# Two alternating parts at the join of layers 1 and 2, and layer 3's norms by a power on GpSimd

## The chip, the cores and the metric

The kernel runs on one core of a Trainium2 chip. The core has TensorE (PE, with its weight loads PEld), VectorE (DVE), ScalarE (ACT) and GpSimd (POOL); SyncE (SP) issues the DMAs. Each engine has its own queue of instructions and takes them in order; semaphores make one wait for another. SBUF holds the tiles, PSUM (eight banks) what PE writes, HBM the rest. The metric is the device time of one launch in microseconds (us), the median of the runs.

## What is computed

Four images of 128 channels and 64 x 64 pixels go through four layers. The parts that the change touches, cut from the reference:

```python
x = x + L0(_gn(x))                 # sorted patches, a scan over 4096 tokens, put back in place
x = x + L1_conv(_gn(x))            # 3x3 convolution of the group norm
t = tokens(x)                      # (B, 4096, 128)
t = t + L2_attn(_ln_t(t))          # 16 heads of 8
t = t + L2_ffn(_ln_t(t))
t = t + L3_attn(_ln_t(t))          # linear attention
t = t + L3_ffn(_ln_t(t))

def L2_attn(x):                    # x is already a layer norm
    q = _qz_ring(heads(x) + rx_theta)
    ctx = softmax(q q^T / sqrt(8)) q
    x1 = _ln(x + ctx @ w_comb.T + b_comb, g1, beta1)
    h = relu((cos(x1[..., :8]) * cos(ry_theta)) @ w1.T + b1)
    return _ln(x1 + h @ w2.T + b2, g2, beta2)

def _ln_t(v, eps=1e-5):
    m, s = mean(v, -1), var(v, -1)
    return (v - m) / sqrt(s + eps)
```

L2_attn's first part, up to `ctx`, is "attention" below; what comes after it, from the division by the softmax's sums to the last norm, is the "feed-forward".

## The kernel before

A batch is held as 128 channels by 4096 tokens and worked through in 8 chunks of 512. Matmuls in float32 go through PE in two passes, so that one line of code can show as two instructions in the trace. Nearly all matmuls have the line of the helper `mm`, L92, and many deferred steps that of `later`, L137; tiles' names tell them apart.

**Order.** Outside two blocks whose order is written out by hand (the scan of layer 0, and the attention of layer 2 for PE, DVE and POOL), a scheduler orders each engine's instructions when the kernel is built: among those that its model holds ready, the one that stands first in the program. A tile waits for its buffer, and a pool opened where another was waits for the tiles that it covers.

**Layers 0 and 1** (`layers01`, from L277). The scan over all batches runs to about 2637 us. Beside it, other batches are prepared or ended. `end` (L1024) is the end of one batch: load the image `xb` in four DMAs, put the scan's output back in place (`put_back`, L962: transposes `perm_t`, matmuls `perm_p` with a permutation, adds into `xb`), then `convolve` (L1001: group norm, 16 pieces of 18 matmuls `conv`, an add each, four stores to `xd`). It is a generator of about 53 turns; `K.flush()` after each turn issues the steps that it deferred, and `K.banks` says how many PSUM banks it may use. The last batch's end runs alone, after the scan, in a pool of eight banks (L1075 to L1081).

**Layer 2** (`layer2_attention`, L1112). First constants: 18 small DMAs on SP and some work on DVE (L1124 to L1183). For each batch then: `prepare` (L1228), in 8 chunks of six stages, `fetch` (load `x_in` from `xd`), `centred` and `norm` (the two halves of a layer norm), `products`, `running` (cosines and their products), `store` (values into `qt` and `value_d`, heads into `head_d`); then `load_steps` reads the first head's keys and queries back in 32 DMAs and POOL rounds them (L1218, L1226). `attention` (L1328) needs all eight PSUM banks and runs its heads one after the other; in each it loads the next head's keys and queries. A part of each head's sums goes to `around_d` by one DMA (L1444). `feed_forward` (L1566) works off the batch before in nine stages a chunk; `fetch` loads `den`, `num` and `nrm_in`, `divisors` (L1609) turns the softmax's sums by matmuls with `pick`, `first_centred` (L1629) adds the residual by a matmul with `center`. The two chunks that need `around_d` come last, and `gathered` (L1584) reads it for each in 16 DMAs of 8 rows. `in_turn` sets the stages of the chunks against each other, and `in_turns` takes one step of each part in each round. For batch b, the feed-forward of b - 1, its `gathered` part, and `prepare(b)` with its loads run together, in this order within a round.

**Layer norm** (`layernorm_steps`, L100). PE centres a chunk; ACT squares it and keeps a copy; PE takes the mean of the squares; DVE transposes (L116); ACT takes the square root (L118); DVE the reciprocal (L119); PE spreads it by transposes (L122); DVE multiplies (L124). ACT holds one table of functions; an `ACT_TABLE_LOAD` comes before a function of another table. `layernorm` (L94) runs all of it in one go and is used by layer 3's attention alone (`norm`, L1999); its chunks go through `norm`, `keys`, `add`, and beside them those of the batch before through `queries`, `weighed`, `give`. The experts' part has another form already: `weigh` adds epsilon on DVE and takes the power -0.5 on POOL (L1796, L1800).

Of the kernel before, what the change touches and what calls it, by code (L numbers as in the profile page):

```python
# [17 lines left out]
P = 128  # L18
# [12 lines left out]
class Common:  # L31
# [62 lines left out]
    def layernorm(self, out, src, work, psum):  # L94


        for _ in self.layernorm_steps(out, [(self.center, src)], work, psum):
            pass

    def layernorm_steps(self, out, terms, work, psum, affine=None, bufs=2):  # L100
# [7 lines left out]
        nc.scalar.activation(sq, xc, AF.Square, bias=shift)  # L108
        kept = work.tile([P, CH], F32, name="ln_kept", bufs=bufs)
        nc.scalar.activation(kept, xc, AF.Identity, bias=shift)  # L110
# [6 lines left out]
        sd = work.tile([P, 4, 1], F32, name="ln_sd")  # L117
        nc.scalar.activation(sd, vt[:, :, 0:1], AF.Sqrt, bias=self.eps5)  # L118
        nc.vector.reciprocal(sd, sd)  # L119
        by_block = vp.rearrange("p (g b i) -> p b g i", b=4, i=32)  # L120
        for k in range(4):
            nc.tensor.transpose(by_block[:, k], sd[:, k].to_broadcast([P, P]), self.ident)  # L122
# [154 lines left out]
def layers01(K, xd, dpool, w, w1):  # L277
# [9 lines left out]
    with ExitStack() as ctx:  # L287
        pool = lambda name, bufs, **kw: ctx.enter_context(tc.tile_pool(reuse_waits="tile", name=name, bufs=bufs, **kw))
        cst = pool("l0_const", 1)
        big = pool("l0_big", 1)  # L290
        small = pool("l0_small", 1)

        norm_g = column(nc, cst, w["norm_g"], "norm_g")
        norm_b = column(nc, cst, w["norm_b"], "norm_b")
        conv1_b = column(nc, cst, w["conv1_b"], "conv1_b")
        conv2_b = column(nc, cst, w["conv2_b"], "conv2_b")
        ca1_wT = matrix(nc, cst, w["ca1_wT"], "ca1_wT")
        ca2_wT = matrix(nc, cst, w["ca2_wT"], "ca2_wT")
        head_w = column(nc, cst, w["head_w"], "head_w")
        head_b = rows(nc, cst, w["head_b"], "head_b")  # L300
        nc.vector.tensor_scalar(head_b, head_b, 0.5, None, ALU.mult)
        z_projT = matrix(nc, cst, w["in_proj_wT"][:, 256:512], "z_projT")
        conv1d_b = column(nc, cst, w["conv1d_b"], "conv1d_b", 2)
        dt_projT = matrix(nc, cst, w["dt_proj_wT"], "dt_projT")
        dt_b = column(nc, cst, w["dt_proj_b"], "dt_b", 2)

        a_neg = cst.tile([P, NQ, NG], F32, name="a_neg")
        for z in range(2):
            for q in range(NQ):
                nc.sync.dma_start(  # L310
                    out=a_neg[64 * z : 64 * z + 64, q, :].unsqueeze(2),
                    in_=w["A_log"][64 * q : 64 * q + 64, :].rearrange("d (g z) -> d g z", z=2)[:, :, z : z + 1],
                )
        d_skip = column(nc, cst, w["D"], "d_skip", 2)
        out_projT = matrix(nc, cst, w["out_proj_wT"], "out_projT", 2)
        taps = cst.tile([P, 9, P], F32, name="taps")
        nc.sync.dma_start(out=taps, in_=w1["weightT"])
        bias = column(nc, cst, w1["bias"], "bias")

        x_projT = cst.tile([P, 2, 80], F32, name="x_projT")  # L320
        nc.vector.memset(x_projT, 0.0)
        for at, rows_ in ((0, slice(0, 24)), (64, slice(24, 40))):
            nc.sync.dma_start(
                out=x_projT[:, :, at : at + rows_.stop - rows_.start],
                in_=w["x_proj_wT"].rearrange("(k p) f -> p k f", k=2)[:, :, rows_],
            )

        row32 = K.shifted("row32_0", K.row_i, 1, (31, None, ALU.bitwise_and))
        state = cst.tile([32, DS], F32, name="state")
        nc.vector.tensor_scalar(state, K.col[0:32, 8 : 8 + DS], row32[0:32], None, ALU.is_equal)  # L330
        c_d = dpool.tile([2, DS, CH], F32, name="c_d")
        image_d = [dpool.tile([P, (HW + 2) * (HW + 2)], F32, name=f"image_d{i}") for i in range(2)]
        y_d = [dpool.tile([P, L], F32, name=f"y_d{b}") for b in range(NB - 2)]

        pair = cst.tile([P, 64], F32, name="pair")
        nc.vector.tensor_tensor(pair, K.ident[:, 0:64], K.ident[:, 64:128], ALU.add)

        in_projT = small.tile([P, 256], F32, name="in_projT", tag="rank_eq")
        nc.sync.dma_start(out=in_projT, in_=w["in_proj_wT"][:, 0:256])
        taps1d = cst.tile([P, 4, 256], F32, name="taps1d")  # L340
        nc.sync.dma_start(out=taps1d, in_=w["conv1d_wT"].partition_broadcast(P))
        nc.vector.tensor_tensor(
            taps1d, taps1d, in_projT.unsqueeze(1).to_broadcast([P, 4, 256]), ALU.mult
        )
        nc.scalar.activation(a_neg, a_neg, AF.Exp)
        nc.vector.tensor_scalar(a_neg, a_neg, -1.0, None, ALU.mult)
        head_bc = cst.tile([P, 64], F32, name="head_bc")
        nc.vector.tensor_scalar(head_bc, K.ones[:, 0:64], head_w, None, ALU.mult)

# [65 lines left out]
        def together(*parts):  # L415

            parts = list(parts)
            while parts:
# [3 lines left out]
                if parts:  # L422
                    yield
# [1738 lines left out]
```

## Time and profile before

| what | us |
|---|---|
| median of the runs (9740.41 to 9745.49) | 9741.62 |
| the profiled execution, its own time | 9744.07 |
| its span, first to last instruction | 9742.2 |
| layers 0 and 1, to the scan's end | 2637 |
| last batch's end, then constants and preparation of batch 0, to the first key load | 2637 to 2847.7 |
| first key load to the first exponential of attention | 2847.7 to 2886.65 |
| attention of batch 0 | 2886.65 to 4168.4 |
| feed-forward of a batch with the next one's preparation, three times | 207, 203, 203 |
| last feed-forward alone | 8627 to 8772 |
| layer 3's attention | 9068 to 9457 |
| granted TensorE clock over the span | 0.927 of full |

A row of the timeline has the start, the length, the engine, the line of code, the instruction, the tile written and the tiles read, the count, and in brackets how long the engine had been idle and what released it. SPq is SP's queue of DMA issues: its lengths are the time to issue, not to land. A row of a line's answer has the count and the shortest, median and longest duration in ns, then the first and last start. Matmuls' ends are modelled.

### The profile page before, as it was taken

Reading aid. Unit: us, or ns where it says so; the run is one execution under the profiler, and the core shown is the slowest. Engines: PE = TensorE matmul, PEld = TensorE weight load, DVE = VectorE, ACT = ScalarE, POOL = GpSimd, SP = SyncE. Lnnn points to the kernel's source line nnn. Section 1 sums busy time; section 2 is a strip of 40 time slices with the busy share of each in tenths; the row PEclk is TensorE's granted clock in tenths of the full one; section 3 lists DMA queues with packets and bytes.
Section 4 is the critical chain, followed back from the end, with each engine's and each line's share of the span. In section 5 each row is a group of like instructions: output and inputs, shape, how many; then the busy total and the mean of one; then the engine's idle time right before and its main releaser. Section 6 shows DMA issues by size and latency. Waiting matters only on the chain.

```text
span 9742.2 us, 188843 instructions
## 1 busy us (share of the span) xinstructions
PE 8688.3 (89%) x74586; PEld 3347.3 (34%) x74586; DVE 7104.0 (73%) x7782; ACT 7404.1 (76%) x10635; POOL 4901.3 (50%) x3255
## 2 busy tenths in 40 slices
PE   5887878889859999979999979999979999987777
PEld 2222222234433333333333333333333333333443
DVE  1889897987738888858888857888867888853454
ACT  3776767654439999969999969999979999972442
POOL 1677676765525555545555545555545555542001
PEclk8887888889879999989999989999989999998898
DMA  4524435222232222142212232222233222224105
GB/s 117 124 72 113 102 80 130 61 66 82 73 73 38 40 39 40 31 109 41 39 40 40 38 96 51 40 39 40 39 91 57 39 40 40 40 57 134 44 10 165
DMA packets 575734, 635.37 MB, mean 65 GB/s; under 512 B 113080, under 2 KB 369152, under 8 KB 573824
## 3 DMA queue, kind: packets, MB, share of 16 engines
q1 hardware_dynamic: 574848, 623.30, 27.4%
q8 instruction: 588, 9.63, 0.4%
q14 instruction: 298, 2.44, 0.1%
HBM read 446.84 MB, written 109.07 MB: 57 GB/s over the span
## 4 chain that ended last, share of the span: by engine, by line
PE 68%; DVE 10%; POOL 7%; ACT 5%; DMA 5%; issue 4%; SPq 1%; DVEq 0%; POOLq 0%; ACTq 0%
PE ctx_ps L92 27%; PE acc_ps L92 14%; PE score L92 11%; DVE hs L919 4%; PE conv L92 4%; POOL hs L923 3%; DVE hs L908 2%; PE y_ps L92 2%; PE ln_xc L92 1%; PE xc_ps L92 1%; PE b_ps L92 1%; DMA w<-in_L_ffn_weight 1%; PE kv L92 1%; ACT decay L915 1%; ACT L915 1%
## 5 line engine op out<-in xcount | busy, mean ns | idle before, releaser
L1542 ACT ACTIVATE ex<-score 128x1024 f32<-128x1024 f32 x5120 | 4925.1, 1036 | 224.6 <-PE score L92 133.2
L92 PE MATMUL ctx_ps<-ex,qt 128*32 128x512 f32 x20480 | 2733.7, 606 | 19.9 <-DVE ctx L1476 19.9
L1491 POOL TENSOR_TENSOR folded<-ex 128x1024 f32<-128x1024 f32 x512 | 1224.0, 2391 | 2100.7 <-ACT ex L1542 1836.1
L1548 DVE STREAM_TRANSPOSE turned<-ex 128x1024 f32<-128x1024 f32 x1536 | 1885.2, 1227 | 335.1 <-ACT ex L1542 334.7
L1524 DVE STREAM_TRANSPOSE turned<-ex 128x1024 f32<-128x1024 f32 x1532 | 1841.8, 1202 | 0.0
L92 PE MATMUL acc_ps<-turned,turned_v 128*32 128x256 f32 x24576 | 1769.5, 379 | 3.1 <-POOL qt L1236 2.3
L919 DVE TENSOR_TENSOR_SCAN hs<-decay,carry,hs 128x512 f32<-128x512 f32 x1024 | 1245.4, 1265 | 196.5 <-ACT decay L915 183.5
L92 PE MATMUL score<-queries,keys 32*128 32x512 f32 x10240 | 1335.4, 497 | 50.0 <-POOL queries L1226 45.3
L92 PEld LDWEIGHTS acc_ps<-turned,turned_v 128*32 128x32 f32 x24576 | 800.9, 110 | 1476.5 <-issue 1324.1
L923 POOL TENSOR_TENSOR hs<-hs,c_sb 128x1024 f32<-128x1024 f32 x512 | 1207.2, 2358 | 70.9 <-DMA c_sb<-c_d 28.6
L915 ACT ACTIVATE decay<-dt,a_neg 128x512 f32<-128x512 f32 x1024 | 693.0, 689 | 656.7 <-DVE hs L919 644.1
L92 PEld LDWEIGHTS score<-queries,keys 32*128 32x128 f32 x10240 | 512.6, 182 | 1145.2 <-ACT ex L1542 780.8
L1354 POOL TENSOR_TENSOR turned_v<-v,quarter 128x1024 f32<-128x1024 f32 x256 | 612.8, 2394 | 264.5 <-PE acc_ps L92 227.1
L92 PE MATMUL y_ps<-hs,pair 128*64 128x512 f32 x2048 | 655.7, 768 | 32.1 <-POOL hs L923 32.1
L1492 POOL TENSOR_TENSOR quarters<-folded 128x512 f32<-128x512 f32 x512 | 658.0, 1285 | 40.2
L92 PEld LDWEIGHTS ctx_ps<-ex,qt 128*32 128x32 f32 x20480 | 406.3, 108 | 654.7 <-issue 598.7
L908 DVE TENSOR_TENSOR hs<-dtx,b_ps 128x2048 f32<-128x2048 f32 x256 | 579.7, 2264 | 54.2 <-PE b_ps L92 30.2
L92 PE MATMUL b_ps<-dbc,state 32*64 32x512 f32 x1024 | 341.2, 748 | 235.0 <-DVE hs L908 234.9
L922 POOL COPY carry<-hs 128x2 f32<-128x2 f32 x512 | 97.9, 191 | 684.0 <-DVE hs L919 665.5
L1542 ACT ACTIVATION_READ_ACCUMULATOR ex<-score 128x1 f32 x2048 | 436.2, 213 | 0.0
L1476 DVE COPY ctx<-ctx_ps 128x512 f32<-128x512 f32 x256 | 176.8, 691 | 329.4 <-PE ctx_ps L92 327.1
L1533 DVE TENSOR_REDUCE dacc<-quarters 128x2 f32<-128x512 f32 x508 | 326.8, 643 | 0.0
(375 smaller groups left out, 8943.8 us busy)
## 6 DMA issues: line engine op xcount, KB each, us to landing
c_sb<-c_d SPq DMA_DIRECT2D x512, 128.0 KB
queries<-head_d SPq DMA_DIRECT2D x1024, 64.0 KB
keys<-head_d SPq DMA_DIRECT2D x1024, 64.0 KB
under<-image_d SPq DMA_DIRECT2D x192, 264.0 KB
dt<-dt SPq DMA_DIRECT2D x128, 256.0 KB
dtx<-dtx SPq DMA_DIRECT2D x128, 256.0 KB
v<-value_d SPq DMA_DIRECT2D x1024, 32.0 KB
w<-in_L_ffn_weight SPq DMA_DIRECT2D x32, 1024.0 KB
```

What stands on the lines that cost most here:

```text
L92: self.nc.tensor.matmul(out, lhsT, rhs, start=start, stop=stop)
L908: nc.vector.tensor_tensor(hs, dtx2, bb.unsqueeze(1).to_broadcast([P, NQ, CH]), ALU.mult)
L915: nc.scalar.activation(ex, dt2[:, q, :], AF.Exp, scale=a_neg[:, q, g : g + 1])
L919: nc.vector.tensor_tensor_scan(hs[:, q, :], decays[q - 2 * i], hs[:, q, :], carry[:, g, q : q + 1], ALU.mult, ALU.add)
L923: nc.gpsimd.tensor_tensor(hs[:, two, :], hs[:, two, :], cs.unsqueeze(1).to_broadcast([P, 2, CH]), ALU.mult)
L1354: nc.gpsimd.tensor_tensor(t, v.unsqueeze(2).to_broadcast([P, 4 * BT, 4, HD]), quarter.unsqueeze(1).to_broadcast([P, 4 * BT, 4, HD]), ALU.mult,
L1491: nc.gpsimd.tensor_tensor(hs, exs[:, :, 0], exs[:, :, 1], ALU.add)
L1492: nc.gpsimd.tensor_tensor(qs, hs[:, :, 0 : CH // 2], hs[:, :, CH // 2 :], ALU.add)
L1524: nc.vector.transpose(*upright)
L1533: nc.vector.tensor_reduce(at, qs, AX.X, ALU.add)
L1542: nc.scalar.activation(ex, sps[p], AF.Exp, scale=scale, accum_out=sums[:, t : t + 1] if summed else None)
L1548: nc.vector.transpose(*upright)
```

## The change

It has five parts. (1) The last batch's end is returned as a generator `last()` and runs alternately with the preparation of batch 0, a turn of the one and a step of the other; each has four PSUM banks, and layer 2's constants and large tiles are taken from the other side of SBUF. The constants now stand before the last batch's end in the program. Loads of the first head come after both. (2) `layernorm` takes the root by `inverse_root`: an add of epsilon on DVE and a power on POOL. (3) The feed-forward adds the residual on DVE (`more`) instead of PE, turns the sums by transposes and a reduction, and its parts come after `prepare` and its loads in a round. (4) `gathered` begins 12 rounds later and reads `around_d` in two DMAs of 120 and 8 rows. (5) For this, the first 15 heads of a batch store to `around_d` in 16 DMAs of 8 rows each.

The diff is large because a `with` block was dissolved and its lines moved to the left; without that:

```diff
-        for _ in self.layernorm_steps(out, [(self.center, src)], work, psum):
+        for _ in self.layernorm_steps(out, [(self.center, src)], work, psum, power=True):
...
-        nc.scalar.activation(sq, xc, AF.Square, bias=shift)
         kept = work.tile([P, CH], F32, name="ln_kept", bufs=bufs)
-        nc.scalar.activation(kept, xc, AF.Identity, bias=shift)
+        if more is not None:
+            nc.vector.scalar_tensor_tensor(kept, xc, shift, more, ALU.add, ALU.add)
+            nc.scalar.activation(sq, kept, AF.Square)
+        else:
+            nc.scalar.activation(sq, xc, AF.Square, bias=shift)
+            nc.scalar.activation(kept, xc, AF.Identity, bias=shift)
...
-        nc.scalar.activation(sd, vt[:, :, 0:1], AF.Sqrt, bias=self.eps5)
-        nc.vector.reciprocal(sd, sd)
+        if power:
+            self.inverse_root(sd, vt[:, :, 0])()
+        else:
+            nc.scalar.activation(sd.unsqueeze(2), vt[:, :, 0:1], AF.Sqrt, bias=self.eps5)
+            nc.vector.reciprocal(sd, sd)
...
-            K.banks = 8
-        with (
-            tc.tile_pool(reuse_waits="tile", name="l0_last", bufs=2) as work,
-            tc.tile_pool(reuse_waits="tile", name="l0_ps", bufs=8, space=PSUM) as psum,
-        ):
+    work = pool("l0_last", 2)
+    psum = pool("l0_ps", 4, space=PSUM)
+    K.banks = 4
-            for _ in end(NB - 1, seqs[NB - 1], work, psum):
-                K.flush()
-            K.flush()
-            K.flush()
+    def last():
+        for _ in end(NB - 1, seqs[NB - 1], work, psum):
+            K.flush()
+            yield
+        K.flush()
+        K.flush()
+    return last(), ctx
...
+def one_by_one(*parts):
+    for part in parts:
+        yield from part
...
-        cst = pool("l2_const", 1)
-        keep = pool("l2_keep", 2)
+        cst = pool("l2_const", 1, side="right")
+        keep = pool("l2_keep", 2, side="right")
...
-                    nc.sync.dma_start(out=around_d[h], in_=accs[h][:, 0].rearrange("p t r -> p (t r)"))
+                    sums = accs[h][:, 0].rearrange("p t r -> p (t r)")
+                    if h + 1 < NH:
+                        for k in range(16):
+                            r = slice(HD * k, HD * k + HD)
+                            nc.sync.dma_start(out=around_d[k, HD * h : HD * h + HD], in_=sums[r])
+                    else:
+                        nc.sync.dma_start(out=around_last_d, in_=sums)
...
-                for h in range(NH):
-                    nc.sync.dma_start(
-                        out=part[HD * h : HD * h + HD],
-                        in_=around_d[h, :, c * P : (c + 1) * P].rearrange("(n d) f -> d n f", d=HD),
-                    )
-                    if h % 4 == 3:
-                        yield
-                yield
+                cols = slice(c * P, (c + 1) * P)
+                r = HD * (NH - 1)
+                nc.sync.dma_start(out=part[0:r], in_=around_d[:, 0:r, cols].rearrange("n q f -> q n f"))
+                nc.sync.dma_start(out=part[r:], in_=around_last_d[:, cols].rearrange("(n d) f -> d n f", d=HD))
+                yield from [None] * 4
...
             def firsts():
+                yield from [None] * 12
...
-                    mm(tp[:, j, :], den[:, j * P : (j + 1) * P], pick)
+                    nc.tensor.transpose(tp[:, j, :], den[:, j * P : (j + 1) * P], K.ident[0 : 2 * NH, 0 : 2 * NH])
                 rd = work.tile([P, 4, NH], F32, name="rd")
-                nc.vector.tensor_tensor(rd, tp, dsum[:, 4 * c : 4 * c + 4], ALU.add)
+                nc.vector.tensor_reduce(rd, tp.rearrange("p j (z h) -> p j h z", z=2), AX.X, ALU.add)
+                nc.vector.tensor_tensor(rd, rd, dsum[:, 4 * c : 4 * c + 4], ALU.add)
...
-                    x1, [(w_comb, num[:, 0]), (K.center, nrm)], work, psum, (b_comb, g1, beta1), bufs=3
+                    x1, [(w_comb, num[:, 0])], work, psum, (b_comb, g1, beta1), bufs=3, more=nrm
...
-                    parts = list(feed_forward(b - 1, past, work, psum)) if b > 0 else []
                     if b < NB:
-                        part, qt, first = prepare(b, big, two, work, psum)
-                        parts.append(part)
+                        stages, loads, qt, first = prepare(b, big, work, psum)
+                    if b == 0:
+                        part, l0_pools = before
+                        run(part, stages)
+                        l0_pools.close()
+                        two = open_(left, "l2_two", 2)
+                        run(loads(two))
+                    else:
+                        two = open_(left, "l2_two", 2)
+                        parts = [one_by_one(stages, loads(two))] if b < NB else []
+                        parts.extend(feed_forward(b - 1, past, work, psum))
                     run(*parts)
```

`inverse_root` (L129) was there before and in no use:

```python
    def inverse_root(self, out, src):
        p, n = out.shape
        self.nc.vector.tensor_scalar(out, src, 1e-5, None, ALU.add)
        return lambda: self.nc.gpsimd.tensor_tensor(out, out, self.minus_half[0:p, 0:n], ALU.pow)
```

## The prediction

> **What bounds the kernel now.** The first view I read is busy time by stretch, around the join of layers 0-1 and layer 2 (columns: stretch, its length, then busy us and count for PE, PEld, DVE, ACT, POOL, then granted TensorE clock, DMA share, GB/s).
>
> ```profile
> 2637.00:2662.00 25.00, 19.36 (x77) 13.82 (x78) 6.54 (x11) 4.11 (x7) 3.24 (x2) 0.73 0.22 82
> 2662.00:2672.00 10.00, 5.66 (x29) 4.69 (x27) 7.41 (x14) 2.46 (x3) 0.51 (x4) 1.00 0.00 0
> 2672.00:2690.00 18.00, 13.31 (x49) 11.36 (x50) 3.90 (x11) 6.01 (x9) 0.00 (x0) 0.72 0.01 1
> 2690.00:2746.00 56.00, 52.68 (x244) 45.74 (x243) 8.16 (x28) 0.00 (x0) 0.00 (x0) 1.00 0.10 38
> 2760.00:2840.00 80.00, 39.61 (x162) 20.50 (x161) 50.77 (x122) 45.05 (x66) 33.17 (x61) 0.59 0.32 101
> 2637.00:2847.70 210.70, 135.20 (x574) 98.33 (x574) 84.65 (x206) 63.46 (x93) 42.42 (x73) 0.74 0.22 69
> ```
>
> The last batch's end is a stage of TensorE: up to 2690 it puts tokens back and waits for the group norm, then the convolution fills PE, with ACT and POOL idle. The first batch's preparation follows, with PE half idle at a clock of 0.59. The whole join, from the scan's end to the first load of keys and queries, takes 210.7 us and no engine is busy over 135 in it.
>
> The second view is the timeline where batch 0's attention gives way to its feed-forward and batch 1's preparation, and the same place for the last feed-forward alone (8627 to 8772).
>
> ```profile
> 4180.32 4.88 SPq L1590 DMA_DIRECT2D around<-around_d  x4
> 4187.85 2.05 PE L92 MATMUL ln_xc<-x_in,center 128*128 128x512 f32 x2 [7.88 <-DMA x_in<-xd]
> 8637.26 6.84 SPq L1590 DMA_DIRECT2D around<-around_d  x8
> 8649.48 1.89 PE L92 MATMUL den_t<-pick,den 32*128 32x16 f32 x8 [8.42 <-DMA den<-den_d]
> ```
>
> Small reads of `around_d` fill SP's queue just where PE waits some 8 us for a load behind them. The chain of waits of this stretch has the same at its head, and loads at its tail (4337 to 4373):
>
> ```profile
> 4177.26 7.29 DMA first_num<-num_d
> 4184.87 5.23 DMA around<-around_d
> 4190.12 5.06 DMA x_in<-xd
> 4349.15 8.94 DMA keys<-head_d
> 4365.05 7.26 DMA queries<-head_d
> ```
>
> The third is layer 3's timeline, one chunk of 10.24 us where two batches run together, with the one kind of power that this trace has:
>
> ```profile
> 9208.69 1.28 ACT L118 ACT_TABLE_LOAD   x1
> 9209.07 0.31 DVE L116 STREAM_TRANSPOSE ln_vt<-ln_var 128x128 f32<-128x128 f32 x1
> 9209.99 0.30 ACT L118 ACTIVATE ln_sd<-ln_vt,eps 128x4 f32<-128x4 f32 x1
> 9210.88 1.28 ACT L2051 ACT_TABLE_LOAD   x1
> 9211.73 0.65 PE L122 MATMUL ln_var<-ident,ln_sd 128*128 128x128 f32 x4 [0.93 <-DVE ln_sd L119]
> L1800 POOL TENSOR_TENSOR ln_sd<-ln_sd,minus_half x32: 1635/1636/1670, 8802.4 to 9552.9; 128x8 f32<-128x8 f32 x32
> ```
>
> The square root and the exponential reload ACT's table twice a chunk, between a transpose and the normalization.
>
> **Part 1, the join.** The work stays; two parts that ran one after the other run together. Of PE's 135.2 us, 91.0 lie before 2746 (sum of the first four rows) and 44.2 are preparation, at clock 0.59. Beside the convolution the clock should be that of its row, 1.00; the preparation's own matmuls (128x512 from `x_in`) take 592 ns at their shortest and 1061 at the median, so 44.2 becomes about 25. PE's sum is 116. Add 10 for the scan's exit chain (2637.95 to 2647.98), in which the preparation still waits for constants, and, as my choice, 17 for matmuls in PE's order that wait for ACT or DVE: 143 instead of 211, a gain of 68. Bounds: 116 + 8 gives 87. At worst each of eight chunks (10.9 us apart alone) meets a piece of convolution (3.8 us) at some five visits to PE and half of that shows, about 20 us a chunk: 13 + 8 x 20 = 173, a gain of 38. I take 68, for PE stands between and the preparation needs only 51 us of DVE, 45 of ACT and 33 of POOL, each with room beside the end's 26, 13 and 4.
>
> What else moves: layer 2's 18 constant loads (8.3 us of SP's issue, 2743.60 to 2751.87) now come before the last batch's four image loads. These issued at 2635.55 and were needed at 2652.93; nothing but they stands behind. A delay of a few us is inside the 17. The preparation's 40 issues (at about 0.35 us) share SP with four stores. Preparation and end have four PSUM banks each instead of eight; a round of the preparation takes four, and the scan ran the end on three. The 39 us from the first key load (2847.69) to the first exponential (2886.65) stay: they are queue and flight, and start when both parts are done.
>
> **Part 2, layer 3's norms.** Removed per chunk: a Sqrt (0.30), a reciprocal (0.17) and both table switches; the window's 64 loads of 1.283 are 82 us of ACT. Added: an add on DVE (0.18, L2064's row) and a power on POOL. The path from the transpose's end (9209.38) to PE's L122 (9211.73) was 2.35; now 0.18 + 1.64 (128x8; for 128x4 no row, so between nothing and this, and I take the row itself) + three hand-overs of 0.06 = 2.0. So 0.3 is gained; and `e_q` no longer waits 1.28 for its table, so its two matmuls (1.72) can go ahead of the keys' on PE; I count a third, 0.55. For 24 chunks 20 us. In the eight chunks of batch 0 alone the table load (1.28) before the key exponential goes and the norm's path grows by 0.5: 6 us. Sum 27. Bounds: PE is busy for 206 of the 254 us of the joint chunks, so 48 + 7 = 55 at most; a loss of 16 if only the 0.5 on the norm's path shows, 32 times.
>
> The Trainium skill ("ScalarE: Activation LUTs", What ACT_TABLE_LOAD costs) counts a drain of 1.38 us with each load of 1.283, 2.66 a switch. In this trace the load of 9210.88 ends at 9212.16 and the next ACTIVATE starts at 9212.17, so no such drain is seen; by the page ACT would be relieved of 170 us, which could only raise the gain to PE's bound.
>
> **Part 3, the feed-forwards.** The 32 reads of `around_d` per batch become 4 and start 12 rounds later; the residual's matmuls (2 x 0.59 on PE) and one of two 0.68 us reads on ACT go, with an add (0.69) on DVE; eight matmul passes with `pick` become four transposes and a small reduction on DVE. The last feed-forward: 8.4 (the wait shown) + 8 x 0.7 of ACT, which paces it = 14. In the three joined stretches (207, 203, 203 us) the head loses 7.9, but preparation and key loads now go first in each round, and the feed-forward, whose banks attention needs, goes last. I take 10 each, 30; bounds 25 (7.9, then 8 chunks of 1.02 and 0.69, and key loads that begin earlier) and a loss of 7. Sum 44, between 89 and a loss of 16.
>
> **Part 4, the stores.** Fifteen heads a batch store `around_d` by 16 instructions instead of one: 60 heads, 15 more issues each. The nearest row, `num_d` (8 rows, 2 KB each), has 0.26; the dearest, `queries`, 0.65: 3.9 to 9.8 us of SP a head. Behind them stand the next head's values, keys and queries. Cover: the last query load of a head was issued by 3165.98 and its cast starts at 3191.57.
>
> ```profile
> 3154.77 11.23 SPq L1218 DMA_DIRECT2D queries<-head_d  x16
> 3191.57 1.91 POOL L1226 CAST queries<-queries 128x2048 fp32r<-128x2048 f32 x1
> ```
>
> 25 us of room, so I count nothing; uncovered it is 60 x 3.9 = 234, at most 588. Late next would be the cast, then the head's first score. The Trainium skill ("DMA: Bandwidth & Descriptors", Rules for kernel authors) speaks against these stores: join small transfers, since under 64 KB overhead prevails, and an outermost dimension below 16 confines a transfer to as many engines; these have 8 KB over 8 rows. No row here has this store. By the rule the queue's time would show, and the sum would be a loss of some 95 us.
>
> **Sum.** 68 + 27 + 44 + 0 = 139. The profiled execution took 9744.07 us (span 9742.2), so 9605; the median of the runs, 9741.62, is 2.5 lower, so 9603. A difference of 0.2%, 19 us, is what runs of this kernel can tell.
>
> **Rivals.** (a) The join doesn't overlap: the order on PE leaves the preparation behind the convolution, and only the constants' 13 us go: 9741.62 - 13 - 27 - 44 = 9658. For it: PE's queue is in order and was full in the convolution; against it: before 2690 PE idles 14.7 us of 53, and over the join 75.5 of 210.7, while the preparation needs nothing that the end makes. (b) The joined feed-forwards gain nothing: key loads ended within 2 us of the feed-forward in the first of them, so relieving one leaves the other; put last, it costs 7 each: 9603 + 30 + 21 = 9654. Both: 9709, or 9722 if the constants' time is not hidden either. (c) The slower side, one mechanism: the stores delay keys and queries past their cast at each head. 139 / 60 = 2.3 us a head cancels the gain, 2.7 makes it slower by 0.2%; at 3.9 it is 9603 + 234 = 9837. Against it stand the 25 us of room.
>
> **Chances.** The forecast 0.65, (a) 0.11, (b) 0.09, both 0.03, (c) 0.12, of which 0.02 lies near no change. Faster by over 0.2%: 0.85; within: 0.05; slower: 0.10. The forecast's own range, parts' bounds not all falling together, is 9540 to 9670; (a) and (b) lie in it, and to take in both together it reaches to 9715.
>
> **What would show it.** First exponential of layer 2 about 68 us earlier than 2886.65, and preparation's matmuls between the convolution's; no Sqrt among layer 3's chunks and a period near 9.4 us; no 8 us PE wait for `x_in` or `den`; attention's 1282 us (2886.65 to 4168.4) unchanged. Wrong if attention grows, if the convolution is broken by PE waits, or if the power takes well over 1.64 us.

## The result, and the profile after

The changed kernel takes 9596.62 us (median of six runs, 9585.31 to 9611.22) against 9741.01 for the kernel before on the same chips (9734.71 to 9745.49). The ratio is 0.9853 with a 95% interval of 0.984 to 0.9865: faster by 144 us, 1.5%. The forecast was 9603 in a range of 9540 to 9715. The profiled execution took 9603.58, its span is 9601.8.

Cut into stages at the same instructions in both traces, the 140.4 us between the two spans lie here. Blocks of attention go from first to last exponential, joined stretches from that to the next block's first; the experts begin where POOL clears `pooled`.

| stage | before | after | gain | forecast |
|---|---|---|---|---|
| to the scan's last y_ps | 2638.5 | 2645.3 | -6.8 | 0 |
| to the first key load (the join) | 211.8 | 147.0 | 64.8 | 68 |
| to the first exponential | 36.4 | 37.9 | -1.5 | 0 |
| attention, four blocks | 5122.8 | 5121.7 | 1.1 | 0 |
| joined feed-forwards, three | 616.5 | 593.8 | 22.7 | 30 |
| last feed-forward | 146.7 | 131.1 | 15.6 | 14 |
| experts of layer 2 | 300.7 | 291.1 | 9.6 | none |
| layer 3's attention | 383.6 | 351.2 | 32.4 | 27 |
| experts of layer 3 | 285.2 | 282.7 | 2.5 | 0 |

The first row is not the change's. Every engine's order of instructions is the same in both kernels up to the last batch's put-back (but for two of DVE at 812 us that start within 5 ns of each other); the changed kernel falls 6 us behind already between 354 and 525 us, where nothing is changed; and over the thirteen profiles of this study with the same scan its end falls anywhere from 2638.0 to 2645.8.

**The join.** The answer to the table of stretches shown before, same columns (length, busy us and count for PE, PEld, DVE, ACT, POOL, clock, DMA share, GB/s):

```profile
2644.00:2667.00 23.00, 16.73 (x62) 11.62 (x63) 6.17 (x28) 5.15 (x9) 4.97 (x5) 0.78 0.44 139
2667.00:2706.00 39.00, 25.49 (x129) 16.25 (x128) 31.29 (x82) 21.80 (x36) 9.40 (x25) 0.75 0.24 78
2706.00:2790.00 84.00, 76.96 (x382) 62.77 (x382) 41.58 (x96) 32.83 (x47) 25.12 (x43) 0.95 0.31 99
2644.00:2792.30 148.30, 120.39 (x574) 91.37 (x574) 79.51 (x205) 59.78 (x90) 39.49 (x73) 0.87 0.31 98
```

PE has the same 574 instructions (by the table's count) in 148 us that it had in 211, and is busy for 120.4 of them, for the preparation's share runs at a clock of 0.95 beside the convolution instead of 0.59 alone. The timeline of PE shows how they mix, pieces of convolution between one chunk's transposes and another's products, without a wait:

```profile
2710.66 1.46 PE L92 MATMUL conv<-xp,taps 128*128 128x256 f32 x6
2711.96 0.60 PE L129 MATMUL ln_var<-ident,ln_sd 128*128 128x128 f32 x4
2712.39 1.89 PE L92 MATMUL conv<-xp,taps 128*128 128x256 f32 x8
2714.12 0.60 PE L1315 MATMUL q_t<-ident,cs 128*128 128x128 f32 x4
2714.56 4.05 PE L92 MATMUL conv<-xp,taps 128*128 128x256 f32 x18
```

**The feed-forwards.** Batch 0's, joined, and the last one, where PE had waited 7.88 and 8.42 us:

```profile
4122.59 1.20 PE L92 MATMUL ln_xc<-x_in,center 128*128 128x512 f32 x2 [4.15 <-DMA x_in<-xd]
4139.46 0.51 SPq L1613 DMA_DIRECT2D around<-around_d  x1
4140.02 4.05 SPq L1614 DMA_DIRECT2D around<-around_last_d  x1
8556.20 0.40 PE L1633 MATMUL den_t<-ident,den 32*128 32x32 f32 x4 [3.09 <-DMA den<-den_d]
```

The waits at the head are 4.15 and 3.09, and the reads of `around_d` stand 20 us behind it. At the tail of the same stretch, SP's queue of issues has something that the forecast did not look at:

```profile
4261.98 0.38 SPq L1323 DMA_DIRECT2D head_d<-part  x1
4271.55 0.34 SPq L1696 DMA_DIRECT2D xd<-x  x1
4271.94 0.68 SPq L1233 DMA_DIRECT2D queries<-head_d  x1
4272.71 11.89 SPq L1233 DMA_DIRECT2D keys<-head_d  x16
```

The last `head_d` that the key loads need is stored at 4261.98, but they follow a store of the feed-forward's, which waited for its `x` until 4271.55.

**Layer 3.** One chunk of 9.43 us where two batches run together (10.24 before):

```profile
9106.55 0.31 DVE L120 STREAM_TRANSPOSE ln_vt<-ln_var 128x128 f32<-128x128 f32 x1
9106.96 0.17 DVE L139 TENSOR_SCALAR ln_sd<-ln_vt 128x4 f32<-128x4 f32 x1
9107.27 1.01 POOL L140 TENSOR_TENSOR ln_sd<-ln_sd,minus_half 128x4 f32<-128x4 f32 x1 [8.43 <-PE q_ps L92]
9108.33 0.41 PEld L129 LDWEIGHTS ln_var<-ident,ln_sd 128*128 128x128 f32 x4 [0.94 <-POOL ln_sd L140]
```

From the transpose's end (9106.86) to PE is 1.47 us instead of 2.35, and the power on four columns takes 1.01.

**The stores.** In a head of attention, SP's issues and the cast that they must come before:

```profile
3167.23 5.34 SPq L1464 DMA_DIRECT2D around_d<-acc  x16
3174.41 7.62 SPq L1233 DMA_DIRECT2D keys<-head_d  x11
3182.07 11.95 SPq L1233 DMA_DIRECT2D queries<-head_d  x16
...
3215.26 1.90 POOL L1241 CAST queries<-queries 128x2048 fp32r<-128x2048 f32 x1
```

Sixteen stores take 5.34 us, and the last query load still goes out 21 us ahead of its cast.

**The images.** And the row of the table with no term in the forecast: the four images that the experts work on. They were issued together before (first line), when the last feed-forward had ended; in the changed kernel they are the lines after it:

```profile
8772.74 2.34 SPq L2101 DMA_DIRECT2D x<-xd  x4
...
8591.69 0.79 SPq L2133 DMA_DIRECT2D x<-xd  x2
8616.63 0.38 SPq L2133 DMA_DIRECT2D x<-xd  x1
...
8678.61 0.32 SPq L2133 DMA_DIRECT2D x<-xd  x1
```

Three of them go out while the last feed-forward runs; by the diff its tiles are on SBUF's right side now, and the images are taken from the left. The fourth needs what the feed-forward stores last.

### The profile page after: what moved, and what is told of

Same layout as the page of the kernel before. It is cut to its first block, busy times and chain, and to the rows that moved or that the text cites. A ratio compares the mean times of both kernels' runs of the same rounds, so it can differ in the third digit from the quotient of the medians.

```text
span 9601.8 us, 189191 instructions
## 1 busy us (share of the span) xinstructions
PE 8629.9 (90%) x74394; PEld 3296.1 (34%) x74394; DVE 7156.8 (75%) x7845; ACT 7287.4 (76%) x10505; POOL 4932.4 (51%) x3287
## 4 chain that ended last, share of the span: by engine, by line
PE 59%; DVE 4%; DMA 3%; POOL 2%; issue 2%; ACT 1%; SPq 1%; DVEq 0%; POOLq 0%; ACTq 0%
PE ctx_ps L92 27%; PE acc_ps L92 14%; PE score L92 12%; PE ln_xc L92 1%; PE kv L92 1%; PE hid_ps L92 1%; DMA w<-in_L_ffn_weight 1%; DMA queries<-head_d 1%; POOL ln_sd L1832 1%; DVE ctx L1498 0%; PE ln_var L129 0%; POOL q L1293 0%; PE pool L92 0%; DVE x L1985 0%; PE tok_t L1888 0%
```

## The experiments

All but the last two start from the changed kernel; times are medians of four runs, and stages are read from each kernel's profile, of one execution. How far such a reading goes can be seen where an edit leaves a stage alone: the changed kernel and experiments 1, 2, 5 and 7 have 590.4 to 596.4 us in the three joined stretches, and with 4 and 9 added, 128.2 to 132.8 in the last feed-forward. Less than some 6 and 5 us there tells nothing.

**1. Layer 3's square root put back.**

```diff
-        for _ in self.layernorm_steps(out, [(self.center, src)], work, psum, power=True):
+        for _ in self.layernorm_steps(out, [(self.center, src)], work, psum):
```

> The changed kernel with the square root on ACT again in layer 3's norms; all else kept. The forecast's part 2 says 27 us, so 9596.6 + 27 = 9624; by the two traces layer 3's attention gained 32.4 us (383.6 to 351.2 from its first normalized chunk to the next stage), so 9629 if nothing else of the change plays into it: the joint chunks' period goes back from 9.43 to 10.24 us, and the stages on either side stay as they are in the changed kernel. Rival: part of the 32 comes from elsewhere (three of the four images now loaded before the stage, another clock); then the period goes back only part of the way and the time is below 9615.

9634.97 us, ratio 0.9889 (0.9875 to 0.9904). Layer 3's attention takes 390.6 us, 39.4 more than changed, the period is 10.24 again, and the other stages stay: the gain of this stage goes with the power, and the rival of other causes falls for the joint chunks. That it is 39 and not the table's 32 comes mostly from where batch 0 runs alone, from the first normalized chunk to the ninth. These are the rows (columns as above) before the change, here, in the changed kernel, and in experiment 4, which has the power and leaves layer 3 as it is:

```profile
9073.40:9159.00 85.60, 58.22 (x242) 39.77 (x242) 22.50 (x53) 42.89 (x65) 0.00 (x0) 0.75 0.00 0
8954.40:9049.00 94.60, 64.66 (x242) 42.48 (x242) 22.56 (x52) 43.30 (x66) 0.00 (x0) 0.68 0.00 0
8967.90:9041.40 73.50, 50.92 (x242) 33.18 (x242) 22.61 (x54) 21.37 (x43) 8.06 (x8) 0.84 0.00 0
8936.40:9021.10 84.70, 64.21 (x242) 40.09 (x242) 22.61 (x55) 22.14 (x43) 8.05 (x8) 0.68 0.00 0
```

With the root it takes 85.6 us at a granted clock of 0.75 and 94.6 at 0.68, with the power 73.5 at 0.84 and 84.7 at 0.68. At the same clock of 0.68 the power is worth 9.9 us here, with the 17.9 to 20.0 of the joint chunks some 28 to 30; the other 10 of the 39 go with the clock. Whether the root lowers the clock is open: both kernels with it have 0.75 and 0.68, ten of the eleven with the power 0.83 to 0.89, and the eleventh 0.68.

**2. The join's two parts one after the other.**

```diff
-                        run(part, stages)
+                        run(part)
+                        run(stages)
```

> The changed kernel with the last batch's end issued as a whole before the preparation, sides of SBUF, banks and places of the constants kept. In the changed kernel the first exponential comes 185 us after the scan's last y_ps, before it came 249 us after. My theory is that the alternation lets PE work in the other part's waits and that constants ahead are worth 13 of these 64 and a first chunk or two some 10 more, since nothing keeps these from PE's idle time before the convolution: first exponential about 225 us after, time 9596.6 + 40 = 9637. Rival 1: the free memory alone does it, and the order in the program hardly matters: under 10 us, below 9607. Rival 2: all of it hangs on the alternation: 64 us, 9660.

9635.89 us, ratio 0.989 (0.9875 to 0.9905); first exponential 222.5 us after the scan's last `y_ps`, where 225 was expected. In the timeline of PE the convolution is one block, and the preparation comes behind it with waits for its own norms:

```profile
2683.77 64.85 PE L92 MATMUL conv<-xp,taps 128*128 128x256 f32 x288
2748.55 0.42 PE L92 MATMUL ln_var<-ln_sq,mean 128*32 128x128 f32 x6
...
2762.22 1.11 PE L129 MATMUL ln_var<-ident,ln_sd 128*128 128x128 f32 x4 [5.03 <-DVE ln_sd L126]
```

So of the 63.3 us by which the first exponential comes earlier after the scan, the alternation is worth 37.6 and the other 25.7 come without it: constants and parts of the preparation's first two chunks now stand ahead of the convolution, in PE's idle time.

**3. One store of `around_d` a head, and small reads.**

```diff
-                    if h + 1 < NH:
-                        for k in range(16):
...
+                    nc.sync.dma_start(out=around_d[h], in_=sums)
...
+                for h in range(NH):
+                    nc.sync.dma_start(
+                        out=part[HD * h : HD * h + HD],
+                        in_=around_d[h, :, c * P : (c + 1) * P].rearrange("(n d) f -> d n f", d=HD),
+                    )
```

> The changed kernel with one store of around_d a head and 16 reads of 8 rows for each of the two chunks, as before the change; the twelve rounds' delay and the order of the parts stay. My theory is that the 16 stores cost nothing in the attention (they take 5.3 us of SP a head, and the last query load is still issued 21 us ahead of its cast), so the attention's blocks stay at 1280 to 1281 us, and that the small reads cost SP 0.7 us each in the feed-forwards, of which in the joined stretches most is hidden by the delay and in the last one, with nothing beside it, some 6 us show: 9597 to 9615. Rival (c) of the forecast: the stores' time on SP shows in each head; then the attention's blocks become shorter than 1280 us and the time falls below 9590.

9628.67 us, ratio 0.9883 (0.9866 to 0.9899). Attention's blocks take 1280.5 to 1281.4 us, so the 16 stores cost nothing, as forecast. The last feed-forward is 5.7 us longer, where 6 was expected; the joined stretches, where I expected most to be hidden, are 213.7, 207.8 and 207.5: 35.2 us more in all, 11.7 each. Two wide reads a chunk instead of 16 are worth more there than the wait at the head that I had counted. The delay of twelve rounds does not hide the small ones: on SP's queue they stand among the stretch's other transfers, from 4128.66 to 4180.26.

**4. The feed-forward first in a round.**

```diff
-                        parts = [one_by_one(stages, loads(two))] if b < NB else []
-                        parts.extend(feed_forward(b - 1, past, work, psum))
+                        parts = list(feed_forward(b - 1, past, work, psum))
+                        parts.extend([one_by_one(stages, loads(two))] if b < NB else [])
```

> The changed kernel with the feed-forward's two parts ahead of the preparation in each round again; all else kept. In the changed kernel the three joined stretches, from the last exponential to the first of the next batch, take 196.1, 198.8 and 198.9 us. The forecast took it that putting the feed-forward last costs at most 7 us a stretch and is worth something at the key loads. By my theory the order is worth about what it costs: stretches within 4 us of these, time 9585 to 9609. Rival (b): being last costs the feed-forward 7 us each time, so that this kernel's stretches are near 191 us and the time 9576. Rival on the other side: the key loads, last in the chain of each stretch, are what the new order brought forward, so the stretches go back to some 204 us and the time is 9614.

9555.63 us, ratio 0.9814 (0.9796 to 0.9831): faster than the change by 41. The joined stretches are 186.0, 187.0 and 190.9, which is 29.9 us less; no other stage of its profile is shorter by more than 2, so where the other 11 come from is open. My theory that the order is worth what it costs falls, and rival (b)'s mechanism holds with 10 us a stretch instead of 7. Key loads did not suffer; SP's queue has them ten us earlier, since the store that stands before them is earlier too:

```profile
4253.40 0.40 SPq L1323 DMA_DIRECT2D head_d<-part  x1
4260.68 0.34 SPq L1696 DMA_DIRECT2D xd<-x  x1
4261.07 0.69 SPq L1233 DMA_DIRECT2D queries<-head_d  x1
```

**5. The images held back.**

```diff
+        if b + 1 < NB:
+            nc.sync.dma_start(out=t[:, 0:1], in_=xd[NB - 1][:, 0:1])
         nc.sync.dma_start(out=t, in_=xd[b])
```

> The changed kernel in which the loads of the first three images for the experts are held back until chunk 0 of the last batch is written, by a 128 x 4 byte load of it into the same tile. In the changed kernel these loads were issued at 8591.69, beside the last feed-forward; before the change all four were issued when it had ended. The stage between the feed-forward and layer 3 took 300.7 us before and 291.1 after, and no term of the forecast has this. My theory is that the 9.6 us are these loads, come free with the tiles on the other side of SBUF: this stage back to about 300 us, all else unchanged, 9597 + 9 = 9606. Rival: the 9.6 us are the granted clock or the experts' own start, and the loads were hidden before as well: stage within 2 us of 291, time 9595 to 9599.

9605.45 us, ratio 0.9861 (0.9846 to 0.9875). The experts' stage takes 303.3 us instead of 291.1 and the others stay (in seven other kernels with the images as in the change it takes 286.3 to 289.6), so the images account for the 9.6 us of the table. PE's wait at the stage's head is put down to the gate's weights, whose load is issued behind the images; its first product with these weights, here and in the changed kernel:

```profile
8688.20 0.69 PE L92 MATMUL gate_ps<-gateT,center 128*128 128x64 f32 x2 [27.86 <-DMA gateT<-in_L_ffn_gate_wT]
8687.57 0.69 PE L92 MATMUL gate_ps<-gateT,center 128*128 128x64 f32 x2 [14.98 <-DMA gateT<-in_L_ffn_gate_wT]
```

From the issue of that load to the product it is 21.2 us here, 20.7 before the change, and 8.6 in the changed kernel. By the whole time, 9 us more than the change's median, the difference is too small for the intervals; the stage carries the reading.

**6. The residual on PE again.**

```diff
-                    x1, [(w_comb, num[:, 0])], work, psum, (b_comb, g1, beta1), bufs=3, more=nrm
+                    x1, [(w_comb, num[:, 0]), (K.center, nrm)], work, psum, (b_comb, g1, beta1), bufs=3
```

> The changed kernel with the residual added by matmuls with center on PE again and the kept copy read by ACT, in place of the add on DVE; all else kept. The forecast counted 0.7 us of ACT for each of the last feed-forward's eight chunks, 5.6 us, and hardly anything in the joined stretches, where PE has 60 us idle of 197: last feed-forward 131 to 137 us, joined stretches as they are, time 9602. Rival: the add on DVE, whose queue is the fuller one in the joined stretches (115 us busy, with 4 to 7 us idle runs before POOL's powers and adds), costs as much as it spares: no difference, or 10 us faster, 9587. Rival on the other side: each of the chunks' 1.2 us of PE and 0.7 of ACT shows in all four stretches: 4 x 8 x 1 = 32 us, 9629.

9605.07 us, ratio 0.9862 (0.9847 to 0.9877). It is the other way round from what I expected: the last feed-forward is as long as with the add (131.6), and the joined stretches are 202.2, 200.4 and 200.8, 9.7 us more in all. ACT did not set the last feed-forward's pace by 0.7 us a chunk.

**7. Each store six times.** Five copies go to a spare tensor.

```diff
                             nc.sync.dma_start(out=around_d[k, HD * h : HD * h + HD], in_=sums[r])
+                            for z in range(5):
+                                nc.sync.dma_start(out=spare_d[z, k, HD * h : HD * h + HD], in_=sums[r])
```

> The changed kernel with every store of around_d written six times: five copies go to a tensor that nobody reads, 80 more issues a head. A head's 16 stores take 5.34 us of SP, and the last query load is issued 21 us before POOL casts it. Five copies more are 27 us of SP. By the forecast's part 4 the room of 21 us takes the first copies, and what goes past it is late at the cast: some 6 us a head beyond 21 where nothing else gives way, 60 x 6 = 360 us, so attention blocks of about 1370 us and a time near 9960; the point from which rival (c) decides lies between one set of stores and six. Rival 1: the stores are spread over the queue's idle times, which hold more than the 21 us, and the attention's blocks stay at 1280 to 1285 us: 9597 to 9615. Rival 2: the transfers themselves are what counts, their 128 bytes to 512 bytes packets filling the DMA engines, and every copy shows: well above 10000.

10302.13 us, ratio 1.0569 (1.0551 to 1.0587): 705.5 us more, 11.8 for each of 60 heads. POOL now waits for what SP issued late:

```profile
3157.46 1.89 POOL L1242 CAST keys<-keys 128x2048 fp32r<-128x2048 f32 x1 [8.92 <-DMA queries<-head_d]
3167.75 1.89 POOL L1242 CAST queries<-queries 128x2048 fp32r<-128x2048 f32 x1 [4.74 <-DMA den_d<-ctx]
```

Rival (c) of the forecast is a real mechanism. The other rival, that the transfers themselves fill the DMA engines, is not what the trace shows: their busy share over batch 0's attention is 0.21 here (2880 to 4275) and 0.20 in the changed kernel (2830 to 4111). A head's 96 stores take 32.4 to 35.9 us of SP (median 34.0), some 29 more than the 5.34 of sixteen, so the room was 29 - 11.8 = 17 us a head, a little under the 21 that the timeline shows between the last issue and the cast; I take it that the difference is the time in which the loads land. My price of 6 us a head was too low by the copies' 2 us more and these 4.

**8. The power in all norms of layer 2.** `power=True` in the three other calls of `layernorm_steps`.

> The changed kernel with the power on POOL also in the norms of the preparation and the feed-forward. The 128x4 power takes 1.007 us, and layer 3's path from the transpose to PE fell from 2.35 to 1.47 us. A joined stretch has 29 table loads (37 us of ACT) and 32 us in which PE waits for ln_sd; without the square root the cosine's table stays. My theory: ACT falls to some 80 us in a joined stretch, each of the 24 norms' paths loses 0.9 us of which half shows: stretches some 10 us shorter each, the last feed-forward, paced by ACT with 14 to 16 loads, some 12 us shorter, the join a few: 9597 - 45 = 9552. Rival: POOL, in order and 98 us busy in a joined stretch with 24 us of powers added, makes the norms wait behind its adds and products: no gain, 9590 to 9610, PE's waits then on POOL's ln_sd instead.

9636.53 us, ratio 0.9892 (0.9877 to 0.9907): 40 us slower than the change. ACT did fall, from 120.8 to 79.9 us in batch 0's joined stretch, but the stretches are 210.9, 210.5 and 211.6 (39.2 more in all) and the last feed-forward 143.7. The waits, longest first, of the changed kernel's stretch and then of this one's (engine and line, released by, us, times, longest):

```profile
PE ln_var L129 <- DVE ln_sd L126: 31.7, 14, 9.8
```

```profile
PEld ln_var L129 <- POOL ln_sd L140: 63.6, 24, 7.4
PE ln_var L129 <- POOL ln_sd L140: 50.6, 22, 7.1
POOL ln_sd L140 <- DVE ln_sd L139: 32.5, 13, 6.1
```

PE waits longer than before, now for POOL, where each power stands in order behind adds and products and itself waits 32.5 us for DVE while others stand behind it. The same edit that paid where POOL was idle costs where it has 98 us of other work.

**9. Three edits together**: the feed-forward first (as in 4), the power in the norms of the first batch's preparation alone, and the fourth image's load moved behind the experts' small loads.

> The changed kernel with three edits in three different stages, each read from its own stage: the feed-forward's parts ahead of the preparation again (joined stretches 187 to 191 us instead of 196 to 199 when alone, about 30 us in all); the power in the norms of the first batch's preparation alone, where POOL is busy 40 of 185 us (scan's end to first exponential 185 us, with the power in all norms 173: I expect some 8 us less than 185); and the fourth image's load behind the experts' small loads (PE waits 15 us there for the gate's weights, of which 8.6 from issue to landing beside 2 MB of image: some 5 us less than 291 in the stage after the feed-forward). Sum 9597 - 30 - 8 - 5 = 9554 by the stages, or 9543 from the 9555.6 that the first edit alone took. Rivals: the power gains nothing in the join, since PE's order and not the norms sets it (stage within 3 us of 185); the gate's weights come no sooner, for the three images before them still fill the DMA engines (stage within 2 us of 291).

9545.92 us, ratio 0.9798 (0.9782 to 0.9814): 51 us faster than the change. Joined stretches 188.0, 189.5 and 188.2. The experts' stage fell to 280.0 (from 291.1, or from the 286.3 to 289.6 of the other kernels), and the gate's product follows its load at once:

```profile
8641.00 0.42 SPq L270 DMA_DIRECT2D gateT<-in_L_ffn_gate_wT  x1
...
8643.14 0.69 PE L92 MATMUL gate_ps<-gateT,center 128*128 128x64 f32 x2 [6.40 <-DMA gateT<-in_L_ffn_gate_wT]
...
8644.09 0.46 SPq L2137 DMA_DIRECT2D x<-xd  x1
```

In the changed kernel, with the fourth image's load ahead of it, the gate's load took from 8678.98 to 8687.57 until PE had it. The power in the join gave little: to the first key load 143.5 us here and in the other three kernels with it 143.5 or 143.6, against 144.8 to 147.0 in the seven with the root and the alternation, some 2 us.

**10. Without the delay.** Experiment 9 without the twelve rounds.

> The three edits, and the reads of around_d without the twelve rounds' delay. By my theory the delay mattered while there were 16 small reads a chunk, which stood on SP ahead of the first x_in; with two wide reads it is worth next to nothing: the joined stretches and the last feed-forward stay within 3 us of those of the three edits. Rival: two reads of 1 MB and 64 KB at the head of a stretch hold up the first x_in, den and num, for which PE then waits, as it did for 8 us before the change: each stretch 4 to 8 us longer, 12 to 30 us in all.

9564.49 us, ratio 0.982 (0.9806 to 0.9835): 18.6 us slower than 9. Joined stretches 190.2, 190.3 and 190.6, 5.3 us more in all, which is within what unchanged stretches differ by, and the last feed-forward 137.7, 6.1 more, which is just outside. I had taken the delay to be worth nothing; the whole time speaks for the rival, and of its place the profile shows the last feed-forward alone. The other 7 to 12.5 of the 18.6 us lie in no stage that I can name (the two profiled executions differ by 5.8).

**11. The feed-forward's stores to `xd` on POOL's queue.** Experiment 9, with

```diff
-                nc.sync.dma_start(out=xd[b][:, c * CH : (c + 1) * CH], in_=x)
+                nc.gpsimd.dma_start(out=xd[b][:, c * CH : (c + 1) * CH], in_=x)
```

> The three edits, and the feed-forward's eight stores to xd issued by POOL, which makes x, instead of SP. In all three kernels looked at the next batch's first key and query loads follow on SP directly upon such a store: the last head_d store that they need was issued 8.4 us (before the change), 9.9 us (changed) and 7.7 us (feed-forward first) earlier. My theory: this store, which waits for POOL's x, holds up the loads, and with it on another queue each joined stretch is some 6 us shorter, 18 us in all. Rival 1: the loads wait for the landing of head_d anyway, or the feed-forward is what ends the stretch: no gain. Rival 2: issuing costs POOL more than SP and delays the chunk's next work: stretches 5 us longer each, last feed-forward up to 8 us longer.

9544.58 us, ratio 0.9799 (0.9784 to 0.9813), the same as 9. The wait is gone:

```profile
4234.66 0.38 SPq L1323 DMA_DIRECT2D head_d<-part  x1
4235.14 0.68 SPq L1233 DMA_DIRECT2D queries<-head_d  x1
```

but the stretches are 185.3, 187.6 and 187.7, 5.2 us less in all instead of 18, which is within what unchanged stretches differ by: rival 1, no gain. For its second half, that the feed-forward's own tail ends the stretch, there is a sign: in all three stretches PE's last step for a norm of the feed-forward starts 0.9 us before the first exponential (2.3 to 7.6 us in experiment 9). By the profile the experts' stage is shorter too, 271.4: the gate's load, no longer behind a waiting store, is issued at 8596.11, 26 us ahead of the stage. The medians don't show it.

## Why the prediction was right, point by point

**Part 1.** Right in mechanism and nearly in size: 64.8 us to the first key load against 68. Of the forecast's terms, PE's sum was 116 and is 120.4, for the clock beside the convolution is 0.95 and not 1.00, and the matmuls before it run at 0.75; the waits were taken as 10 + 17 and are 27.9. What the forecast had wrong is the division: it credited the alternation with all but the constants' 13 us, and experiment 2 shows 25.7 that come without it, where tiles, banks and the constants' places are the change's and the scheduler does the rest. Rival (a) was priced with 13 us left of the join; without the alternation 25.7 are left.

**Part 2.** 27 was forecast, 32.4 came, 39.4 by experiment 1, of which 28 to 30 at an equal clock. In the joint chunks the sum was right (period 9.43, forecast about 9.4), but by two errors that cancel. The power was taken at its 128x8 row, 1.64, so that only 0.3 of the norm's path was credited; at 1.01 the path fell by 0.88, which is all of the 0.81 that the period lost. By this sum nothing is left for the third of 1.72 that I gave to `e_q`; no run takes the two apart. The joint chunks gained 20.0, as forecast. The rest is batch 0's eight chunks alone, 0.8 forecast each: from the first normalized chunk to the ninth they took 85.6 us before and 73.5 after (9041.42 - 8967.93), 1.5 each, at a granted clock of 0.75 and 0.84; at the same clock (experiments 1 and 4) it is 1.2.

**Part 3.** Here a step failed, though its sum came near (38.3 against 44). The last feed-forward's 14 was 15.6, but not through its second half: experiment 6 shows nothing of the 8 x 0.7 of ACT. By experiments 3 and 10 the reads give some 5.7 and the delay some 6.1, each just beyond what the stage varies by. In the joined stretches the sentence "preparation and key loads now go first in each round" was held to balance the feed-forward's going last; it costs 10 us a stretch (experiment 4), and the wide reads, which I counted with the head's 7.9, give 11.7 (experiment 3). Undone one at a time, 35.2 for reads, -29.9 for the order and 9.7 for the residual, and some 5 for the delay (measured with the feed-forward first, experiment 10, and within the noise), sum to 20 of the 22.7; such parts need not add, and the transposes in place of the matmuls with `pick` were not undone. So the term was too large because one half of the change took back what the other half gave. The lower bound, a loss of 16 for the whole part, does not follow from the terms as given: three losses of 7 and a gain of 14 are a loss of 7.

**Part 4.** Right: nothing in attention. By the page of the Trainium skill that spoke against the stores ("DMA: Bandwidth & Descriptors", Rules for kernel authors) the forecast would have been a loss of 95 us; 8 KB stores show no time here, because SP has room ahead of the cast. The page's rule, to join small transfers, fits the queue's time, 5.34 us a head where one store took 0.34 (experiment 3), and the other side of the same edit, where 32 small reads in place of four wide ones cost 11.7 us a stretch. What decides is whether somebody waits behind.

**The sum, and what no term had.** The four terms came to 135.5 us of the 139 forecast. That the whole came so near is in part luck: outside the terms stand the scan's -6.8 and the images' 9.6, and they nearly cancel. The 9.6 us of the images (experiment 5) were in the change and in no term. The diff shows the move to the right side; I read it for what it frees in the join and did not ask what else takes the tiles that become free.

## What to carry to other kernels

When a change reorders parts that share an in-order queue, find the first transfer of the next stage and what stands just ahead of it there: a store that waits for another part's result can hold up loads that have long been ready, though taking it away gains only where those loads end the stage (experiment 11 gained nothing clear). A part that ends the stage should not go last in each round: here that cost 10 us a stretch. Replacing one engine's operation by another's is priced at the place: the same power gained 28 to 39 us where GpSimd was idle, by the clock that one counts in, and lost 52 in the feed-forwards where it had work queued. When tiles move, ask of every later pool which loads may now start sooner, not only of the stage for which they were moved.

## What the runs showed of the hardware

The power on GpSimd takes 1.006 us on 128x4 and 1.636 on 128x8 (medians), so by these two shapes about 0.16 us for each further element of a partition over a base of 0.38: the price taken from the other shape was off by 0.63 us, nearly two thirds of the real one. The granted clock of one and the same stretch, where layer 3 runs batch 0 alone, was 0.84 in the changed kernel's profile and 0.68 in that of experiment 4, which does not touch it, and its eight chunks took 73.5 us and 84.7: 11 us in a stage with the same instructions. The first key load to the first exponential, which is 32 loads and their flight, took 28.9 to 39.5 us in kernels that don't differ there. And the scan's end, in the same order of instructions, varied by 8 us over thirteen profiles.
